# The third product ordered ahead of a chunk's sums, and a new order for a layer's first step, in a three-layer WKV kernel with a graph convolution

## The chip, the cores and the metric

The kernel runs on one core of one Trainium2 chip. The metric is the time of one execution on the device, in microseconds. Five engines work beside each other, each through its own queue of instructions in order: TensorE (PE in the profile) multiplies matrices, VectorE (DVE) and GpSimd (POOL) work elementwise, ScalarE (ACT) evaluates functions, SyncE (SP) issues the transfers. An engine waits on semaphores where it needs another's result.

## The reference, cut to what matters

The input x has 16 images of 192 channels and 56 x 56 positions, in 32-bit floats. Three layers of the first kind follow each other, then one convolution layer. All four add their result to x, and all start with a group norm (32 groups of 6 channels).

```python
# one layer of the first kind; xs is the normed x as tokens (T = 3136) by channels
k = xs @ Wk.T; v = xs @ Wv.T; r = xs @ Wr.T
x_fwd = wkv_scan(-exp(w_decay), u, k, v)            # over the tokens, forwards
x_bwd = flip(wkv_scan(-exp(w_decay), u, flip(k), flip(v)))   # and backwards
h = sigmoid(r) * 0.5 * (x_fwd + x_bwd)
h = (h - mean(h)) * rsqrt(var(h) + 1e-5) * ln_g + ln_b       # over the channels
x = x + h @ Wo.T

# wkv_scan, in the form without the running maximum:
#   q_t = d * q_{t-1} + e^{k_t};  p_t = d * p_{t-1} + e^{k_t} v_t    (d = e^w)
#   y_t = (p_t + c e^{k_t} v_t) / (q_t + c e^{k_t})

# the last layer
m = max(x[2 up] - x, x[2 down] - x, x[2 left] - x, x[2 right] - x, 0)
x = x + gelu(batch_norm(conv_w @ concat(x, m) + conv_b))
```

## The kernel before, in words

**Tiling.** Two images make a pair: 2 x 192 channels are three blocks of 128 rows (the middle one holds the remaining 64 channels of both images). The tokens are cut into seven chunks of 448. So a tile of a chunk is 128 x 3 x 448. The tiles live in 33 slots that are handed out and given back in program order. Matrix results live in seven PSUM banks, which are handed out in the same way. A product of a 384-channel chunk with a weight matrix (`project`, L597 to L607) takes three banks.

**Two passes.** A layer goes over its pair twice. The pass forwards (unit "A") does, for a chunk: k (`a_keys`), e^k (`a_exp`), v (`a_values`), e^k v (`a_ekv`), the scans of q and p (`a_q`, `a_p`, L875), the bonuses, which add c e^k and c e^k v (`a_den`, `a_num`, L890), the inverse of the denominator as ln and exp(-.) on ScalarE (`invert`, L975 and L978), and y on POOL (`a_y`, L982). The pass backwards (unit "B") takes the chunks from the last to the first: scans (`b_q`, `b_p`), bonuses (`b_den`, `b_num`, L890), inverse, and on POOL the mix (`b_mix`, L1031 to L1033, nine multiplies and adds, three for each block), which joins both directions and multiplies by sigmoid(r). For the sigmoid, r is a product (`b_gate`), then e^-r on ScalarE (`b_exp`, L996), then ln and exp (`b_sigmoid`, L1003 and L978).

**The layer norm behind the mix**, for a chunk: squares on ScalarE (`b_squares`, L1040); sums over the channels as matmuls into one bank (`b_sums`, L1047 for the outer blocks, L1049 for the middle one); the squared mean on ScalarE (`b_rs1`, L1055); its subtraction as a matmul (`b_rs2`, L1059); ln and exp on ScalarE (`b_rs3`, L1063 and L1065); the spreading of the result over the rows by matmul (`b_spread`, L1071); the scaling on VectorE (`b_scale`, L1076); the product with Wo (`b_out`, "ops"); its addition to x (`b_x`, L1089) and a store; and the statistics for the next layer's norm on ScalarE (`b_stats`, L734 and L735).

**Order of the work.** The order of each engine's queue is that of the program: the whole is under a manual schedule. Two streams of pairs are interlaced, so that in most steps the backward chunk of one pair and the forward chunk of the other are worked on together. A list of 249 steps is made, and each calls one function:

- `both_a`, here called a joint step, 85 times: a backward chunk b and a forward chunk a. A chunk's layer norm is spread over two steps: squares, sums and L1055 at the end of a joint step, L1059 on in the next one.
- `both_a_first`, the opening step, 17 times: the first such step after the turn between two layers. It finishes the layer norm of the last chunk before it in full, and begins that of its own.
- `forward_a` and `backward_alone`, at the turn between layers. In `backward_alone` stands `gap(G)`, which takes the next part of the following layer's group norm from a list: here `norm_fold`, four small operations on POOL, and the folding of the norm into the weights of k and v on ScalarE (L770).
- `both_c` (42) and `forward_c`: the same with the convolution, in 7 groups of six `both_c` each.

One opening step and the five joint steps after it are called a group here. There are 17. In nine of them the steps also carry the count of statistics of the input of later pairs (`count`: one or two blocks per step, two passes of ScalarE with an accumulation each, L734 and L735): these are called counting groups, the other eight quiet groups.

**Where r stands.** A step gets the next step's backward chunk as `nback` and calls `b_gate(nback)` and then `b_exp(nback)`; in `both_a` these are the first two calls. So TensorE's queue in a joint step is: r, L1059, v, L1071, ops, k, sums. ScalarE's queue, from the sums on, is: L1055, ln and exp of q (`invert(den())`), then the next step's e^-r, counting, the saving of a column (`b_q`, L884), L1063, L1065, sigmoid, the inverse of b's denominator, statistics, squares and e^k.

Of the kernel before, what the change touches and what calls it, by code (L numbers as in the profile page):

```python
# [55 lines left out]
NL = T // L  # L56
# [417 lines left out]
def fast_path(ctx: ExitStack, tc: tile.TileContext, flag, x, wproj, wfold, wcfold, wconst, wgroup, sums, picks, vecs, out):  # L474
# [374 lines left out]
    def product(run, what, w, xs, first):  # L849

        ps = run.ps[what] = banks(what)
        n = L + 1 if first else L
        project(ps, w, lambda rows, j: xs.full[rows, j, 0:n], n)
# [81 lines left out]
    def a_ekv(run, c):  # L935
        if c == 0:
            take_bias(run, "v", V)
        e, ps, b = slot_of(run.ekv, c, "ekv"), run.ps["v"], run.bias["v"]
        for j in ORDER:
            V.scalar_tensor_tensor(e.t[:, j, :], ps[j][:, 0:L], b[:, j, :], run.ek[c].t[:, j, :], ALU.add, ALU.mult)  # L940
            release(ps[j])

    def a_q(run, c):
        if once(run, "q", c):
            run.den[c] = scan(run, "q", run.ek[c], AHEAD, c == 0)
# [38 lines left out]


    def b_gate(run, c):
        product(run, "r", run.w[2], run.xb[c], c == NL - 1)

    def b_exp(run, c):
        if c == NL - 1:  # L990
# [21 lines left out]
    def b_den(run, c):  # L1012
        q = run.q.pop(c)
        bonus(run, run.ek[c], run.ek[c], q)
        q.give(V)

    def b_p(run, c):
        if c not in run.p:
            run.p[c] = scan(run, "p", run.ekv[c], BACK, c == NL - 1)
            if c > 0:  # L1020
                save(run.p[c], BACK, run.ekv[c - 1])
# [15 lines left out]
    def b_squares(run, c, js=ORDER):  # L1037
        h, sq = run.h[c].t, run.ek[c].t
        for j in js:
            S.activation(sq[:, j, :], h[:, j, :], AF.Square)  # L1040

    def b_sums(run, c):
        h, sq = run.h[c].t, run.ek.pop(c)
        st = run.ps["st"] = bank("st")
        parts = ((h, 0), (h, 1), (sq.t, 0), (sq.t, 1))
        for n, (t, i) in enumerate(parts):
            PE.matmul(st[32 * n : 32 * n + 32, :L], ones[:, 0, :], t[:, 2 * i, :], start=True, stop=False)  # L1047
        for n, (t, i) in enumerate(parts):
            PE.matmul(st[32 * n : 32 * n + 32, :L], ones[:, 1 + i, :], t[:, 1, :], start=False, stop=n < 2)  # L1049
        sq.give(PE)  # L1050

    def b_rs1(run, c):
        rs, st = row.tile([P, L], F32, tag="rs", name=name("rs")), run.ps["st"]
        run.rs[c] = rs
        S.activation(rs[LO, :], st[LO, :L], AF.Square)  # L1055

    def b_rs2(run, c):

        PE.matmul(run.ps["st"][HI, :L], pick[LO, 0, 0:64], run.rs[c][LO, :], start=False, stop=True)  # L1059
# [260 lines left out]
        for _ in range(min(most, len(z))):  # L1320
            z_stats(*z.pop(0))

    def both_a(b, a, nback, nfront, z, loads):

        den = lambda: a[0].den[a[1]]
        l = of_stage(0.5)
        load_ahead(nback)
        store()
        if nback is not None:
            b_gate(*nback[1:])  # L1330
            b_exp(*nback[1:])
        count(z)
        b_q(*b)
        if l:
            b_rs2(*l)
            b_rs3(*l)
        b_sigmoid(*b)
        a_values(*a)
        if l:
            b_spread(*l)  # L1340
        b_p(*b)
        b_den(*b)
        for js in (AC, slice(1, 2)):
            ln(b[0].ek[b[1]], js)
            exp_minus(b[0].ek[b[1]], js)
        b_num(*b)
        b_mix(*b)
        for u in loads:
            load_ahead(u)
        if l:  # L1350
            b_scale(*l)
            b_out(*l)
            late[l] = 2
        a_ekv(*a)
        sum_up()
        keys(nfront)
        a_q(*a)
        if l:
            add(l)
        b_squares(*b, (0,))  # L1360
        a_save(*a)
        count(z)
        exp_keys(nfront, (0, 2))
        b_squares(*b, (2,))
        exp_keys(nfront, (1,))
        b_squares(*b, (1,))
        b_sums(*b)
        a_p(*a)
        gap()
        a_den(*a)  # L1370
        b_rs1(*b)
        late[b] = 0.5
        invert(den())
        gap()
        a_num(*a)
        a_y(*a)
        gap()

    def both_a_first(b, a, nback, nfront, loads):

        den = lambda: a[0].den[a[1]]
        l = of_stage(0)
        load_ahead(nback)
        store()
        a_values(*a)
        b_squares(*l, (0, 2))
        b_q(*b)
        b_sigmoid(*b)
        b_p(*b)
        b_den(*b)  # L1390
        invert(b[0].ek[b[1]])
        b_num(*b)
        b_mix(*b)
        for u in loads:
            load_ahead(u)
        a_ekv(*a)
        b_squares(*l, (1,))
        if nback is not None:
            b_gate(*nback[1:])
        b_sums(*l)  # L1400
        b_rs1(*l)
        if nback is not None:
            b_exp(*nback[1:])
        a_q(*a)
        b_rs2(*l)
        b_rs3(*l)
        keys(nfront)
        a_p(*a)
        spread_and_scale(l)
        b_squares(*b, (0,))  # L1410
        a_save(*a)
        exp_keys(nfront)
        b_squares(*b, (2, 1))
        b_sums(*b)
        a_den(*a)
        b_rs1(*b)
        late[b] = 0.5
        invert(den())
        a_num(*a)
        add(l)  # L1420
        a_y(*a)
# [245 lines left out]
    def backward_alone(b, nback, nfront):  # L1667
        load_ahead(nback)
        load_ahead(nfront)
        store()  # L1670
        sum_up()
        b_q(*b)
        gap()
        b_den(*b)
        gap()
        invert(b[0].ek[b[1]])
        b_sigmoid(*b)
        b_p(*b)
        gap(G)
        b_num(*b)  # L1680
        b_mix(*b)
        for u in list(late):
            finish(u)
        if nback is not None:
            b_gate(*nback[1:])
            b_exp(*nback[1:])
        keys(nfront)
        exp_keys(nfront)
        late[b] = 0
# [13 lines left out]
    with tc.manual_schedule(engines={PE.engine, V.engine, S.engine, G.engine, nc.sync.engine}):  # L1703
        S.preload_act_table_set(TABLES)
        first = chains[0][0]
        for c in range(NL):
            load_ahead(("Z", first, c))
        for c in range(NL):
            count([(first, c, j) for j in ORDER], 3)
        for i, (b, f, z) in enumerate(steps):  # L1710
            nback, nfront, _ = steps[i + 1] if i + 1 < len(steps) else (None, None, None)
            for run in starts.get(i, ()):
                begin_later(run)
            if i == 0:
                keys(f)
                exp_keys(f)
            ahead = [("Z", run, c) for run, c, _ in (z if not b else [])]
            ahead += [nfront] if b and f else []
            ahead += [("Z", run, c) for run, c, _ in (steps[i + 1][2] if i + 1 < len(steps) else [])]
            ahead += [steps[i + 2][0]] if i + 2 < len(steps) else []  # L1720

            nkeys = nfront if nfront is not None and nfront[0] == "A" else None
            if f and not b and nkeys is None and nfront is not None and i + 2 < len(steps):
                far = steps[i + 2]
                if far[0] is None and far[1] is not None and far[1][0] == "A" and far[1][1] is f[1]:
                    nkeys = far[1]
            if f and nback is None and nfront is not None:
                near = [u for _, u, _ in steps[i + 1 : i + 4] if u is not None and u[0] == "A"]
                if len(near) > 1 and near[1][1] is near[0][1]:
                    ahead.append(near[1])  # L1730
            if not (b and f):
                for u in ahead:
                    load_ahead(u)
            if b and f and f[0] == "A":
                if of_stage(0) is None:
                    both_a(b[1:], f[1:], nback, nfront, z, ahead)
                else:
                    both_a_first(b[1:], f[1:], nback, nfront, ahead)
            elif b and f:
                both_c(b[1:], f[1:], nback, nfront, ahead)  # L1740
            elif f and f[0] == "A":
                forward_a(f[1:], nback, nfront, nkeys, z)
            elif f:
                forward_c(f[1:], nback, nfront)
            elif b:
                backward_alone(b[1:], nback, nfront)
            else:
                neither(nback, nfront)
            assert not z
        store()  # L1750
        assert not late and not unsummed and not convs and not half
# [100 lines left out]
```

## Time and profile before

| | us |
|---|---|
| median of 3 runs | 5206.31 |
| lowest and highest | 5205.58, 5208.39 |
| the profiled execution | 5220.16 |
| its span, first to last instruction | 5218.2 |

| steps of one group, from the start of the backward scan of q on VectorE | quiet group, us | counting group, us |
|---|---|---|
| opening step | 30.5 | 30.5 |
| first joint step | 25.7 | 27.0 |
| second, third, fourth | 23.6, 23.6, 23.6 | 26.6, 27.2, 27.2 |
| fifth | 24.3 | 24.2 |

The mean granted TensorE clock is 0.935 of full speed. A line of the timeline has the start in us, the duration in us from the first to the last of the instructions merged in it, the engine, the line of the program, the operation, out<-in, the sizes, and in brackets the idle time of the engine before it and what ended that. A line of the windows view has a stretch of the span, its length, the busy time of each engine with the number of its instructions, the granted share of TensorE's clock (PEclk), and the share of the DMA engines. An engine that is never idle in a step sets the step's length; where none is, the step is set by a loop through several engines.

### The profile page before, as it was taken

How to read it: one execution, taken by the hardware profiler on the slowest of the kernel's cores; microseconds unless marked ns; L12 is line 12 of the kernel's file. 1: busy time of each engine (PE TensorE's matmuls, PEld its weight loads, DVE VectorE, ACT ScalarE, POOL GpSimd, SP SyncE). 2: the span in 40 equal slices, each digit the busy share in tenths (PEclk: the TensorE clock that was granted, in tenths of full speed). 3: DMA queues.
4: the chain of work that ended last, by engine and by line, in shares of the span. 5: the costliest groups of instructions: out<-in, count | busy, mean ns of one | idle time of the engine just before them, and what ended most of it. 6: DMA issues, size and time to landing. Idle time of an engine off the chain costs nothing. (4 is left out here: it accounts for less than half of the span.)

```text
span 5218.2 us, 51856 instructions
## 1 busy us (share of the span) xinstructions
PE 4733.3 (91%) x15542; PEld 1498.8 (29%) x15542; DVE 4750.5 (91%) x6271; ACT 3684.6 (71%) x7163; POOL 2889.2 (55%) x2251
## 2 busy tenths in 40 slices
PE   7899998989899999998989999999898999999897
PEld 3222222223232222222323222222232322222222
DVE  6999999998989999999898999999889899999995
ACT  6777787776566777787656678777756667777772
POOL 1665665554545656565454556556545455666562
PEclk8999999999899999999989999999998999999998
DMA  5222222233232222223233223222333322222233
GB/s 154 69 82 87 90 86 89 85 110 97 90 116 72 87 90 93 82 90 122 93 93 101 84 75 100 88 85 87 128 93 101 93 74 77 72 84 77 80 104 120
DMA packets 314274, 482.47 MB, mean 92 GB/s; under 512 B 66432, under 2 KB 306688, under 8 KB 313984
## 3 DMA queue, kind: packets, MB, share of 16 engines
q1 hardware_dynamic: 312832, 477.59, 28.5%
q8 instruction: 126, 2.06, 0.2%
q10 hardware_dynamic: 1152, 1.48, 0.1%
q14 instruction: 164, 1.34, 0.1%
HBM read 324.83 MB, written 154.14 MB: 92 GB/s over the span
## 5 line engine op out<-in xcount | busy, mean ns | idle before, releaser
L875 DVE TENSOR_TENSOR_SCAN q<-fdecays,ek 128x449 f32<-128x449 f32 (+1 forms) x1008 | 1023.4, 1068 | 28.0 <-ACT ek L920 25.4
L875 DVE TENSOR_TENSOR_SCAN p<-fdecays,ekv 128x449 f32<-128x449 f32 (+1 forms) x1008 | 1020.3, 1065 | 0.6
L982 POOL TENSOR_TENSOR p<-p,q 128x1344 f32<-128x1344 f32 x168 | 512.0, 3047 | 830.3 <-ACT q L978 546.9
L1031 POOL TENSOR_TENSOR ekv<-ekv,ek 128x448 f32<-128x448 f32 x504 | 602.7, 1196 | 456.1 <-ACT ek L978 385.3
L1033 POOL TENSOR_TENSOR p<-p,sg 128x448 f32<-128x448 f32 x504 | 638.0, 1266 | 57.2 <-ACT ek L884 12.7
L1032 POOL TENSOR_TENSOR p<-p,ekv 128x448 f32<-128x448 f32 x504 | 606.1, 1203 | 39.5
L1040 ACT ACTIVATE ek<-p 128x448 f32<-128x448 f32 x504 | 286.4, 572 | 309.4 <-POOL p L1033 308.9
L886 POOL COPY ekv<-p 128x3 f32<-128x3 f32 x282 | 233.1, 827 | 488.0 <-DVE p L875 457.2
L1076 DVE TENSOR_TENSOR p<-p,rsb 128x448 f32<-128x448 f32 x504 | 282.4, 613 | 194.5 <-PE rsb L1071 194.4
L920 ACT ACTIVATE ek<-k,k 128x448 f32<-128x448 f32 x504 | 297.2, 632 | 225.3 <-PE k L601 179.2
L735 ACT ACTIVATE fjunk<-x 128x448 f32<-128x448 f32 x672 | 387.7, 577 | 40.1 <-DVE x L1089 13.4
L1071 PE MATMUL rsb<-rs,fpicks 32*128 32x448 f32 (+1 forms) x1008 | 359.2, 629 | 42.4 <-ACT rs L1065 42.4
L1159 POOL TENSOR_TENSOR ml<-ml,x 128x1344 f32<-128x1344 f32 x56 | 178.9, 3194 | 391.8 <-ACT ml L1150 391.8
L890 DVE SCALAR_TENSOR_TENSOR ek<-ek,fcc,q 128x896 f32<-128x896 f32 x336 | 379.1, 1167 | 0.0
L890 DVE SCALAR_TENSOR_TENSOR q<-ek,fcc,q 128x896 f32<-128x896 f32 x336 | 359.2, 1109 | 6.3 <-ACT cvb L954 4.6
L1089 DVE SCALAR_TENSOR_TENSOR x<-ops,fwob,x 128x448 f32<-128x448 f32 x504 | 314.2, 670 | 46.7 <-PE ops L601 26.6
L734 ACT ACTIVATE fjunk<-x 128x448 f32<-128x448 f32 x600 | 342.5, 571 | 11.4
L996 ACT ACTIVATE sg<-r,r 128x448 f32<-128x448 f32 x504 | 313.0, 627 | 33.5 <-PE r L607 20.7
L890 DVE SCALAR_TENSOR_TENSOR ekv<-ekv,fcc,p 128x896 f32<-128x896 f32 x336 | 330.1, 1022 | 0.0
L940 DVE SCALAR_TENSOR_TENSOR ekv<-v,v,ek 128x448 f32<-128x448 f32 x504 | 312.5, 672 | 16.6 <-PE v L601 8.0
L975 ACT ACTIVATE q<-q 128x1344 f32<-128x1344 f32 x168 | 221.5, 1318 | 125.5 <-DVE q L890 101.3
L890 DVE SCALAR_TENSOR_TENSOR p<-ekv,fcc,p 128x896 f32<-128x896 f32 x336 | 295.3, 919 | 6.5 <-POOL ekv L886 1.7
(235 smaller groups left out, 11546.4 us busy)
## 6 DMA issues: line engine op xcount, KB each, us to landing
x<-xd SPq DMA_DIRECT2D x240, 672.0 KB, 5.3
xd<-x SPq DMA_DIRECT2D x168, 672.0 KB, 3.9
x<-in_x_dram SPq DMA_DIRECT2D x320, 224.0 KB, 4.3
x<-in_x_dram SPq DMA_DIRECT2D x320, 112.0 KB, 4.2
out_dram<-ml SPq DMA_DIRECT2D x112, 224.0 KB, 2.3
m<-xd SPq DMA_DIRECT2D x112, 168.0 KB, 5.1
wkv<-in_wfold_dram SPq DMA_DIRECT2D x24, 640.0 KB, 5.6
out_dram<-ml SPq DMA_DIRECT2D x112, 112.0 KB, 2.3
```

Source lines behind the costliest of these rows:

```text
L734: S.activation(junk, xt[:, j, :], AF.Identity, accum_out=stats[:, 0, j, c : c + 1])
L735: S.activation(junk, xt[:, j, :], AF.Square, accum_out=stats[:, 1, j, c : c + 1])
L875: V.tensor_tensor_scan(out, dec[:, column(j)].to_broadcast([P, L if first else L + 1]), e, 0.0, ALU.mult, ALU.add)
L890: by_channel(lambda js, i: V.scalar_tensor_tensor(dst.t[:, js, :], e.t[:, js, :], cc[:, i : i + 1], state.t[:, js, :], ALU.mult, ALU.add))
L940: V.scalar_tensor_tensor(e.t[:, j, :], ps[j][:, 0:L], b[:, j, :], run.ek[c].t[:, j, :], ALU.add, ALU.mult)
L982: G.tensor_mul(run.h[c].t, run.h[c].t, den.t)
L996: S.activation(sg.t[:, j, :], ps[j][:, 0:L], AF.Exp, bias=b[:, j, :], scale=-1.0, accum_out=run.chk[:, at : at + 1])
L1031: G.tensor_mul(y.t[:, j, :], y.t[:, j, :], den.t[:, j, :])
L1032: G.tensor_add(h.t[:, j, :], h.t[:, j, :], y.t[:, j, :])
L1033: G.tensor_mul(h.t[:, j, :], h.t[:, j, :], sg.t[:, j, :])
L1071: PE.matmul(ps[j][:, :L], pick[rows, j, :], rs[rows, :], start=True, stop=True)
L1089: V.scalar_tensor_tensor(xj, ps[j][:, 0:L], wob[:, column(j)], xj, ALU.add, ALU.add, accum_out=run.new[:, 0, j, c : c + 1] if c == 0 else ...
```

## The change

No operation is added or taken away. Four things change places.

1. In `both_a` and `both_a_first`, the product r of the backward chunk two steps on (`far`, if it is of the same layer and pair) is put just ahead of the step's own sums. The next step's call of `b_gate` then does nothing for it, since `once` remembers it. Each group's r of four chunks is concerned; the r that the opening step makes for its own `nback` stays where it was.
2. In the opening step, `a_q` and `a_ekv` (with the squares of the middle block after them) go ahead of the bonuses of the backward chunk.
3. Also there, L1059 to L1065 (`b_rs2`, `b_rs3`) go ahead of e^-r, the saving of q's column ahead of `a_p`, and spreading, scaling and ops (`spread_and_scale`) ahead of k (`keys`).
4. In `backward_alone`, `gap(G)` goes from behind sigmoid and the scan of p to ahead of both.

In the main loop a name is changed (`then`) and `far` is worked out. All lines from L988 on move down by one, those after the opening step by more.

```diff
     def b_gate(run, c):
-        product(run, "r", run.w[2], run.xb[c], c == NL - 1)
+        if once(run, "r", c):
+            product(run, "r", run.w[2], run.xb[c], c == NL - 1)
...
-    def both_a(b, a, nback, nfront, z, loads):
+    def both_a(b, a, nback, nfront, z, loads, far):
...
         exp_keys(nfront, (1,))
         b_squares(*b, (1,))
+        if far:
+            b_gate(*far[1:])
         b_sums(*b)
         a_p(*a)
...
-    def both_a_first(b, a, nback, nfront, loads):
+    def both_a_first(b, a, nback, nfront, loads, far):
...
         b_q(*b)
         b_sigmoid(*b)
         b_p(*b)
+        a_q(*a)
+        a_ekv(*a)
+        b_squares(*l, (1,))
         b_den(*b)
         invert(b[0].ek[b[1]])
         b_num(*b)
         b_mix(*b)
         for u in loads:
             load_ahead(u)
-        a_ekv(*a)
-        b_squares(*l, (1,))
         if nback is not None:
             b_gate(*nback[1:])
         b_sums(*l)
         b_rs1(*l)
+        b_rs2(*l)
+        b_rs3(*l)
         if nback is not None:
             b_exp(*nback[1:])
-        a_q(*a)
-        b_rs2(*l)
-        b_rs3(*l)
-        keys(nfront)
+        a_save(*a)
         a_p(*a)
         spread_and_scale(l)
+        keys(nfront)
         b_squares(*b, (0,))
-        a_save(*a)
         exp_keys(nfront)
         b_squares(*b, (2, 1))
+        if far:
+            b_gate(*far[1:])
         b_sums(*b)
         a_den(*a)
         b_rs1(*b)
...
         invert(b[0].ek[b[1]])
+        gap(G)
         b_sigmoid(*b)
         b_p(*b)
-        gap(G)
         b_num(*b)
         b_mix(*b)
...
+            far = steps[i + 2][0] if nback is not None and i + 2 < len(steps) else None
+            if far is not None and far[1] is not nback[1]:
+                far = None
             if b and f and f[0] == "A":
                 if of_stage(0) is None:
-                    both_a(b[1:], f[1:], nback, nfront, z, ahead)
+                    both_a(b[1:], f[1:], nback, nfront, z, ahead, far)
                 else:
-                    both_a_first(b[1:], f[1:], nback, nfront, ahead)
+                    both_a_first(b[1:], f[1:], nback, nfront, ahead, far)
```

More of the change, by code (lines that the diff above doesn't have):

```diff
@@ L1723, in fast_path @@
             if f and not b and nkeys is None and nfront is not None and i + 2 < len(steps):
-                far = steps[i + 2]
-                if far[0] is None and far[1] is not None and far[1][0] == "A" and far[1][1] is f[1]:
-                    nkeys = far[1]
+                then = steps[i + 2]
+                if then[0] is None and then[1] is not None and then[1][0] == "A" and then[1][1] is f[1]:
+                    nkeys = then[1]
             if f and nback is None and nfront is not None:
```

## The prediction

> **What bounds the kernel now.** I read the page's busy times first, then busy time step by step, then the timelines of one quiet step, one counting step and one opening step. The page:
>
> ```profile
> PE 4733.3 (91%) x15542; PEld 1498.8 (29%) x15542; DVE 4750.5 (91%) x6271; ACT 3684.6 (71%) x7163; POOL 2889.2 (55%) x2251
> ```
>
> Two engines at 91% can't say which one sets a step. The windows view, cut where VectorE starts its first backward scan of a step, does: a quiet joint step, the opening step, and the first and third joint step of a counting group.
>
> ```profile
> core 0: us, PE busy (x) PEld busy (x) DVE busy (x) ACT busy (x) POOL busy (x), PEclk, DMA share, GB/s
> 412.50:436.10 23.60, 23.29 (x82) 7.15 (x84) 23.60 (x31) 19.25 (x38) 15.32 (x12) 1.00 0.27 89
> ...
> 512.80:543.30 30.50, 28.37 (x110) 8.97 (x110) 27.14 (x32) 19.86 (x40) 23.39 (x24) 1.00 0.02 7
> 543.30:570.30 27.00, 24.91 (x88) 7.57 (x82) 25.65 (x30) 21.59 (x46) 17.67 (x15) 0.95 0.38 128
> ...
> 596.90:624.10 27.20, 25.11 (x82) 7.64 (x80) 25.09 (x31) 21.59 (x45) 15.67 (x12) 0.94 0.22 77
> ```
>
> A quiet joint step is full on VectorE (23.60 of 23.60) and all but full on TensorE: nothing can be won there, only lost. A counting step has 2.1 us free on both: a loop through several engines sets it. The loop, in the quiet step's timeline:
>
> ```profile
> 409.15 0.94 PE L1049 MATMUL st<-p,fsums 128*32 128x448 f32 x4 [0.30 <-POOL p L1033]
> ...
> 410.63 1.02 PE L598 MATMUL r<-x,wr 128*128 128x448 f32 x2
> 410.75 0.54 ACT L1055 ACTIVATE rs<-st 64x448 f32<-64x448 f32 x1 [1.05 <-PE st L1049]
> ...
> 413.77 0.62 ACT L996 ACTIVATE sg<-r,r 128x448 f32<-128x448 f32 x1
> ...
> 415.14 0.96 PE L1059 MATMUL st<-rs,fpicks 64*64 64x448 f32 x2
> ...
> 416.80 0.57 ACT L1065 ACTIVATE rs<-rs 64x448 f32<-64x448 f32 x1
> ...
> 420.54 1.97 PE L1071 MATMUL rsb<-rs,fpicks 32*128 32x448 f32 x6
> ...
> 421.99 1.14 POOL L1031 TENSOR_TENSOR ekv<-ekv,ek 128x448 f32<-128x448 f32 x1 [2.42 <-ACT ek L978]
> ...
> 422.43 1.02 PE L598 MATMUL ops<-p,fwo 128*128 128x448 f32 x2
> ```
>
> Sums, then r (4.51 us, 410.63 to 415.14), then L1059. While r runs, ScalarE does L1055, ln and exp of q, and e^-r, all ahead of L1063 and L1065. So r hides that chain from TensorE. The mix of POOL then runs 421.99 to 432.7 and ends as VectorE starts its bonuses. In a counting step 1.4 us of counting stands on ScalarE in this loop, and the mix comes later:
>
> ```profile
> 565.65 2.59 DVE L890 SCALAR_TENSOR_TENSOR q<-ek,fcc,q 128x896 f32<-128x896 f32 x2
> 565.73 2.04 POOL L1033 TENSOR_TENSOR p<-p,sg 128x448 f32<-128x448 f32 x1
> ...
> 567.82 0.96 PE L1049 MATMUL st<-p,fsums 128*32 128x448 f32 x2 [2.09 <-POOL p L1033]
> ```
>
> The bonus takes 2.59 where it took 1.72 in the quiet step (409.18), the POOL multiply 2.04 where it took 1.15. TensorE waits 2.09, and then runs at half clock:
>
> ```profile
> 567.70:571.10 3.40, 3.28 (x10) 1.00 (x11) 3.32 (x4) 1.50 (x3) 3.40 (x5) 0.50 0.01 2
> ```
>
> Last, the opening step:
>
> ```profile
> 518.72 3.15 DVE L890 SCALAR_TENSOR_TENSOR ek<-ek,fcc,q 128x896 f32<-128x896 f32 x2
> ...
> 536.63 1.68 DVE L1076 TENSOR_TENSOR p<-p,rsb 128x448 f32<-128x448 f32 x3 [3.36 <-PE rsb L1071]
> ```
>
> Bonuses doubled by the mix beside them, then 3.36 us of waiting for the spreading, which stands behind k (4.5 us) on TensorE.
>
> [...]
>
> **The change part by part.** No instruction is added or removed; only order changes. Times inside a joint step are counted from the start of ops.
>
> *r ahead of the sums, joint steps.* TensorE's order becomes rs2, v, spreading, ops, k, r, sums. ops, k and r are 13.53; the sums unbroken take 1.78 to L1055 (527.81 to 529.59 in the opening step): L1055 at 15.31. From there ScalarE needs 3.02 to e^-r (410.75 to 413.77), 1.85 for that, 1.48 for saving and L1063/L1065: 6.35, now with only rs2 and v (5.5) to cover it. Then 1.11 to the scaling (spreading to first scaling 1.05) and 0.73 to ops: 23.50 a step, beside VectorE's 23.58. But the mix starts 4.62 after L1065 (393.81 to 398.43), which is 2.8 after ops where it was 0.4 before ops, and takes 10.66: it ends at 13.4, and the bonuses start at 10.31 (scaling 398.12 to bonus 409.18, less 0.73). So 3.1 us of mix lies on them. From the counting step, 1.15 of POOL work beside a bonus costs VectorE 0.87 and POOL 0.89, so I take 0.75 per us on VectorE and, with 0.5 in the opening step (1.87, 1.52, 1.88 and 1.41 for four times 1.14), 0.65 on POOL. Settling the period against this overlap: 25.8, 25.5, 25.2 in the second to fourth step, for 23.58: over the group +1.9, +1.6, +1.2. Lower bound: no collision, 23.58. Counting steps: 1.41 more in the chain, collision full, the mix ends at 15.4, L1055 at 17.1, period 17.1+6.35+1.41+1.84 = 26.7 for 26.6, 27.2, 27.2: -1.1 over three steps; without collision 24.9. The waits left (0.7, 1.7, 1.0) are shorter than 2.09, so I give the clock back. The fourth step has no r left; its mix sets it still. Fifth: 0 quiet, +1.7 counting (mix now on the bonuses).
>
> *Banks and loads.* The moved r takes banks freed by b_x and by e^k, both done before k ends; its x is loaded some 15 us ahead. Nothing, either way at most 0.5.
>
> *Folding ahead of p.* k starts 2.75 after r because the fold (1.73) stands behind two sigmoid passes (2.67). Now k starts at 511.5, not 514.3; sigmoid is 1.7 later, POOL needs it at 515.2 as it comes.
>
> *Opening step.* v ends at 521.0; r, sums to 527.2. The scan of q and e^k v now stand ahead of the bonuses on VectorE, which are then free of the mix (-3.2) but end b_den at 525.6 for 521.9. Its ln/exp on ScalarE ends 528.3, and L1055 stands behind it: rs2 528.8, L1065 531.05, scaling 532.2 for 536.6, ops 532.9 for 537.5. Then k, and r of two chunks on: 546.5, sums, L1055 548.3 (before 543.8, with that r after it). L1065 of the next step: 554.65, scaling 555.8 (counting 557.2) for 554.6. With the mix then on its bonuses (+2.2) the first joint step ends 572.5 for 569.0: +3.5 quiet, 573.9 for 570.3: +3.6 counting. VectorE's own gain of 2.4 in the opening step is spent in waiting there.
>
> *Convolution groups.* The same fold move lets mix and sums come about 1.4 earlier in the first step of 7 groups: -10.
>
> *Sum.* 8 quiet groups: 3.5+1.9+1.6+1.2 = 8.2, 66. 9 counting groups: 3.6-1.1+1.7 = 4.2, 38. Less 10: +94 on the profiled 5220.2 (span 5218.2), thus 5314 there. The median is 5206.3, 0.27% lower: 5300.
>
> **Rivals.** (a) The collision doesn't come, because VectorE's pace lets the mix slip ahead again. For it: before, the mix ended just where the bonuses began. Against: the mix hangs on L1065, as the scaling does, so it can't gain on ops. Then quiet groups lose 1.3 (10), counting ones gain 5.5 (50), folding 10: 5156. It decides from an overlap below some 1 us a step. (b) TensorE's new waits in counting groups pull the clock to half in four steps each: 4x9x1.7 = 61 more, 5360. Against: each is shorter than 2.09. (c) Gain and loss meet, overlap about half of mine: 5206 within 0.2%, for which 10 us is what a measurement of this kernel can tell.
>
> **How the numbers follow.** Forecast 0.62, (a) 0.20, (b) 0.10, (c) 0.08. Slower 0.72, same 0.08, faster 0.20. The likeliest one's own range is 5240 to 5340; with (b), (c) and part of (a) 5170 to 5360.
>
> **What would show it.** Right: quiet joint steps of about 25 us with bonuses (L890) of 2.3 to 2.9 beside L1034, the new name of L1033; gaps on TensorE before rs2 (0.7) and before the spreading; first joint steps with several us of VectorE idle ahead of the scaling; PEclk at 1.00 in counting steps. Wrong: quiet steps still at 23.6, or counting ones below 25.5.

## The result, and the profile after

| | us |
|---|---|
| before, median | 5205.94 (5199.82 to 5208.39) |
| after, median of 4 runs | 5411.84 (5405.23 to 5422.42) |
| ratio, with its 95% interval | 1.0399 (1.0380 to 1.0418) |
| span of the profiled execution, before and after | 5218.2, 5409.3 |

The change makes the kernel 206 us slower. The forecast was 94 us slower, and 5411.84 lies outside its range of 5170 to 5360. The busy line of the page after:

```profile
PE 4794.1 (89%) x15542; PEld 1516.8 (28%) x15542; DVE 4828.1 (89%) x6271; ACT 3671.6 (68%) x7163; POOL 2840.4 (53%) x2251
```

Same instructions, but VectorE is busy 78 us longer (4750.5 before) and TensorE 61 us (4733.3 before): part of the loss is work that runs slower, the rest is waiting. POOL is busy for less time (2889.2 before).

The profiled execution of the kernel before was 14 us longer than its median, which is why the spans differ by 191 us and the medians by 206. Cutting both traces at the start of the backward scan of q, step by step, shows where the 191 us are. The table gives after minus before for one group, as a mean over the 8 quiet and the 9 counting groups, beside the prediction's own terms.

| step | quiet, measured | quiet, predicted | counting, measured | counting, predicted |
|---|---|---|---|---|
| opening and first joint step | +0.9 and +7.9 | +3.5 | +1.0 and +8.7 | +3.6 |
| second, third and fourth | +0.7, +3.8, +3.1 | +1.9, +1.6, +1.2 | -0.6, -0.1, +0.5 | -1.1 together |
| fifth | -0.4 | 0 | +0.4 | +1.7 |

The groups make +218 (8 x 16.0 and 9 x 9.9); the convolution steps give back 11.6, the forward steps at the turns 15.4. So the first joint steps alone hold 63.5 + 78.5 = 142, more than the whole forecast.

The windows view of after, from the start of one step to that of the next: the third and fourth quiet step; an opening step, and the stretch in the middle of it; the first joint step behind it; then the second to fifth joint step of that counting group together.

```profile
435.60:462.90 27.30, 24.59 (x83) 7.61 (x84) 27.30 (x30) 19.03 (x37) 15.18 (x12) 0.94 0.23 76
462.90:489.90 27.00, 22.08 (x88) 6.25 (x84) 27.00 (x30) 20.44 (x39) 15.22 (x12) 1.00 0.21 71
...
541.60:572.50 30.90, 27.72 (x84) 8.77 (x84) 24.83 (x33) 17.06 (x33) 21.72 (x21) 0.83 0.13 45
...
558.60:568.80 10.20, 9.14 (x15) 3.16 (x16) 4.15 (x6) 3.61 (x10) 9.74 (x10) 0.50 0.00 0
...
572.50:607.30 34.80, 31.96 (x120) 9.49 (x116) 25.41 (x31) 24.61 (x52) 16.52 (x15) 1.00 0.30 100
...
607.30:712.20 104.90, 94.03 (x300) 29.16 (x300) 101.54 (x118) 85.55 (x176) 61.77 (x48) 0.90 0.28 92
```

The quiet steps are again full on VectorE, 27.00 of 27.00, with the same operations that took 23.60 before: its operations have become slower. The opening step has a stretch of 10.2 us in which TensorE is granted half its clock (0.83 over the step, 1.00 before), and VectorE is busy only 24.83 of 30.90. In the first joint step VectorE is idle for 9.4 us.

The timeline of the fourth quiet step, with the lines of VectorE's slow operations and of what set their neighbours:

```profile
458.75 2.61 DVE L890 SCALAR_TENSOR_TENSOR q<-ek,fcc,q 128x896 f32<-128x896 f32 x2
...
465.25 0.54 ACT L1056 ACTIVATE rs<-st 64x448 f32<-64x448 f32 x1 [4.83 <-PE st L1050]
465.69 1.31 ACT L975 ACTIVATE q<-q 128x1344 f32<-128x1344 f32 x1
...
467.04 1.33 ACT L978 ACTIVATE q<-q 128x1344 f32<-128x1344 f32 x1
...
468.50 3.05 POOL L982 TENSOR_TENSOR p<-p,q 128x1344 f32<-128x1344 f32 x1 [7.69 <-ACT q L978]
...
468.85 4.24 DVE L890 SCALAR_TENSOR_TENSOR ek<-ek,fcc,q 128x896 f32<-128x896 f32 x2
...
476.18 1.14 POOL L1032 TENSOR_TENSOR ekv<-ekv,ek 128x448 f32<-128x448 f32 x1 [3.64 <-ACT ek L978]
...
485.72 2.65 DVE L890 SCALAR_TENSOR_TENSOR q<-ek,fcc,q 128x896 f32<-128x896 f32 x2
```

The denominator of q was ready at 461.36 (458.75 + 2.61), yet its inverse (L975, L978) starts at 465.69: it stands behind L1056, which waits 4.83 for the sums, because r now runs ahead of them. The inverse sets POOL's y (L982), which at 468.50 falls on the backward bonuses. They take 4.24 where they took 1.71 before. The mix (L1032) comes late as well, behind sigmoid and the inverse in ScalarE's queue, and makes the forward bonuses 2.65 long. In the kernel before, in the same step (it begins at 436.06), y ran beside the two scans and was over before the bonuses began:

```profile
437.56 3.05 POOL L982 TENSOR_TENSOR p<-p,q 128x1344 f32<-128x1344 f32 x1 [3.64 <-ACT q L978]
439.02 3.02 DVE L875 TENSOR_TENSOR_SCAN p<-fdecays,ekv 128x449 f32<-128x449 f32 x3
441.98 1.71 DVE L890 SCALAR_TENSOR_TENSOR ek<-ek,fcc,q 128x896 f32<-128x896 f32 x2
```

The opening step of a counting group and the start of the next, in the timeline:

```profile
555.57 1.33 ACT L978 ACTIVATE ek<-ek 128x1344 f32<-128x1344 f32 x1
556.80 0.52 ACT L1056 ACTIVATE rs<-st 64x448 f32<-64x448 f32 x1
...
557.38 0.96 PE L1060 MATMUL st<-rs,fpicks 64*64 64x448 f32 x2 [1.86 <-ACT rs L1056]
...
559.66 3.72 PE L1072 MATMUL rsb<-rs,fpicks 32*128 32x448 f32 x6 [1.32 <-ACT rs L1066]
...
563.32 1.86 PE L598 MATMUL ops<-p,fwo 128*128 128x448 f32 x2
...
566.38 0.21 ACT L884 ACTIVATE ek<-q 128x3 f32<-128x3 f32 x1 [4.79 <-POOL p L1033]
...
589.97 1.69 DVE L1077 TENSOR_TENSOR p<-p,rsb 128x448 f32<-128x448 f32 x3 [8.22 <-PE rsb L1072]
```

L1056 starts as the inverse ahead of it ends, 1.3 after the sums. TensorE waits 1.86 for it, does L1060, and waits again, 1.32, since k no longer stands between L1060 and the spreading. From there it runs at half clock: the spreading takes 3.72 instead of 1.97, ops 7.2 (563.32 to 570.52) instead of 4.58, some 4.3 us lost. Then come k, r and the sums, so in the next step VectorE waits 8.22 for its scaling.

### The profile page after: what moved, and what is told of

The parts are those of the page before. It is cut to its first block, busy times and chain, and to the rows that moved or that the text cites. A ratio compares the mean times of both kernels' runs of the same rounds, so it can differ in the third digit from the quotient of the medians.

```text
span 5409.3 us, 51930 instructions
## 1 busy us (share of the span) xinstructions
PE 4794.1 (89%) x15542; PEld 1516.8 (28%) x15542; DVE 4828.1 (89%) x6271; ACT 3671.6 (68%) x7163; POOL 2840.4 (53%) x2251
## 5 line engine op out<-in xcount | busy, mean ns | idle before, releaser
L982 POOL TENSOR_TENSOR p<-p,q 128x1344 f32<-128x1344 f32 x168 | 519.4, 3091 | 1082.0 <-ACT q L978 776.6
L875 DVE TENSOR_TENSOR_SCAN p<-fdecays,ekv 128x449 f32<-128x449 f32 (+1 forms) x1008 | 1022.3, 1070 | 43.2 <-PE st L1050 42.6
L875 DVE TENSOR_TENSOR_SCAN q<-fdecays,ek 128x449 f32<-128x449 f32 (+1 forms) x1008 | 1024.7, 1072 | 23.5 <-ACT ek L920 20.9
L1032 POOL TENSOR_TENSOR ekv<-ekv,ek 128x448 f32<-128x448 f32 x504 | 598.6, 1188 | 512.3 <-ACT ek L978 428.0
L1034 POOL TENSOR_TENSOR p<-p,sg 128x448 f32<-128x448 f32 x504 | 614.2, 1219 | 59.0 <-ACT sg L978 13.9
L1033 POOL TENSOR_TENSOR p<-p,ekv 128x448 f32<-128x448 f32 x504 | 618.1, 1226 | 39.5
L1072 PE MATMUL rsb<-rs,fpicks 32*128 32x448 f32 (+1 forms) x1008 | 391.5, 673 | 131.8 <-ACT rs L1066 131.8
L890 DVE SCALAR_TENSOR_TENSOR q<-ek,fcc,q 128x896 f32<-128x896 f32 x336 | 411.9, 1267 | 39.0 <-ACT ek L884 34.4
L890 DVE SCALAR_TENSOR_TENSOR ek<-ek,fcc,q 128x896 f32<-128x896 f32 x336 | 430.6, 1322 | 0.0
L886 POOL COPY ekv<-p 128x3 f32<-128x3 f32 x282 | 202.4, 718 | 317.7 <-DVE p L875 300.5
L890 DVE SCALAR_TENSOR_TENSOR p<-ekv,fcc,p 128x896 f32<-128x896 f32 x336 | 297.4, 927 | 44.5 <-POOL ekv L886 41.3
L598 PE MATMUL ops<-p,fwo 128*128 128x448 f32 x336 | 233.3, 785 | 113.1 <-DVE p L1077 112.6
L940 DVE SCALAR_TENSOR_TENSOR ekv<-v,v,ek 128x448 f32<-128x448 f32 x504 | 312.8, 675 | 11.6 <-PE v L601 8.0
L1060 PE MATMUL st<-rs,fpicks 64*64 64x448 f32 x336 | 174.4, 601 | 151.5 <-ACT rs L1056 142.6
```

The source lines that it names most:

```text
L875: V.tensor_tensor_scan(out, dec[:, column(j)].to_broadcast([P, L if first else L + 1]), e, 0.0, ALU.mult, ALU.add)
L890: by_channel(lambda js, i: V.scalar_tensor_tensor(dst.t[:, js, :], e.t[:, js, :], cc[:, i : i + 1], state.t[:, js, :], ALU.mult, ALU.add))
L982: G.tensor_mul(run.h[c].t, run.h[c].t, den.t)
L1032: G.tensor_mul(y.t[:, j, :], y.t[:, j, :], den.t[:, j, :])
L1033: G.tensor_add(h.t[:, j, :], h.t[:, j, :], y.t[:, j, :])
L1034: G.tensor_mul(h.t[:, j, :], h.t[:, j, :], sg.t[:, j, :])
```

## The experiments

Each was compared with the kernel before on the same chip, and the ratio to that is given with its 95% interval. Differences by step are taken from the profiled spans.

### The parts by themselves

The changed kernel without part 1 (r where it was):

```diff
-        if far:
-            b_gate(*far[1:])
         b_sums(*b)
```

> The changed kernel with r where it was before (parts 2, 3 and 4 alone). Theory A: the opening step's new order makes TensorE wait twice (1.86 and 1.32 us) and so run spreading and ops at half clock, whatever r does; the first joint step then comes some 4.3 us late in each of 17 groups (73 us) less some 10 us for the fold: about 5270 us, with spreading near 3.7 us and ops near 7.2 us in the opening step. Theory B: r ahead of the sums is the whole cost: 5190 us or less, with spreading near 2.0 and ops near 4.6 us.

Measured: 5290.97, 1.0142 (1.0118 to 1.0167). Its windows: a quiet joint step, an opening step, and 10.2 us in the middle of that.

```profile
423.90:447.40 23.50, 23.21 (x82) 7.07 (x82) 23.50 (x30) 19.24 (x37) 15.29 (x12) 1.00 0.27 87
523.00:553.90 30.90, 27.70 (x84) 8.69 (x84) 24.81 (x33) 17.10 (x33) 21.75 (x21) 0.83 0.14 45
...
539.90:550.10 10.20, 9.00 (x15) 3.02 (x16) 4.15 (x6) 3.75 (x10) 9.74 (x10) 0.50 0.00 0
```

Without the moved r, quiet joint steps are back at 23.6, but the half clock in the opening step is there as in the changed kernel. So the half clock comes from the opening step's new order, the long quiet steps from r. First joint steps are still 5.0 (quiet) and 5.9 (counting) longer than before. Theory B falls.

Part 1 alone, on the kernel before (the `far` lines of both step functions and of the main loop, `once` in `b_gate`, nothing else):

> The kernel before with r of two chunks on ahead of the sums alone (part 1). Theory A: r costs 3.5 us in the first joint step (no half clock, as the old opening step has no two waits) and what the later joint steps of the changed kernel show (7.6 us in quiet groups, about 0 in counting ones): 8 x 11 + 9 x 3.5, about 5320 us. Theory B, r is the whole cost: 5410 us.

Measured: 5312.75, 1.0186 (1.0161 to 1.0210). The window of a fourth quiet step of it:

```profile
454.90:481.90 27.00, 23.65 (x88) 6.75 (x84) 27.00 (x30) 20.47 (x39) 15.23 (x12) 0.94 0.22 70
```

It has the 27.0 of the changed kernel, and its opening step keeps most of its clock (0.95 over the step). Its first joint steps are 4 longer. So r costs by itself some 2%, and theory B falls here too.

Part 4 alone (the fold of the norm ahead of sigmoid and p):

```diff
+        gap(G)
         b_sigmoid(*b)
         b_p(*b)
-        gap(G)
```

> The kernel before with the folding ahead of sigmoid and p alone (part 4). The steps of the convolution and the forward steps behind them lose 27 us in the changed kernel; if the fold does this, about 5180 to 5190 us. If the fold only moves k ahead of work that sets the pace anyway: 5206 us.

Measured: 5165.48, 0.9897 (0.9870 to 0.9924). This part is a gain of 54.5 on the spans, more than either expectation: 20.4 in the opening steps, of which many are 29.5 long instead of 30.5, some 10 in the joint steps, 12.4 in the convolution groups and 14.2 in the forward steps at the turns. The last two aren't shown to be the fold's: in the run of part 1 alone, which has no fold, the convolution groups are 6.3 and the forward steps 17.3 shorter than in the same trace of the kernel before.

On the spans, the fold is worth -54.5, r by itself +87.8 (5306.0), parts 2 and 3 +127.3 (5291.0 against 5163.7). That is +160.6, and 30.5 less than the change. They aren't a cost of the parts' meeting each other: within the groups the fold is worth -30.6, r +113.7, parts 2 and 3 +134.7, together 217.8, and the changed kernel has 217.6. The 30.5 lie outside the groups, in convolution steps and turns, where the trace of the kernel before is longer than those of all the other runs, so that much the same 25 us are counted as a gain of the fold and again as a gain of r.

### What costs in the opening step

The changed kernel, with r moved in joint steps only:

```diff
         b_squares(*b, (2, 1))
-        if far:
-            b_gate(*far[1:])
         b_sums(*b)
```

> The changed kernel with r moved in the joint steps alone, not in the opening step. Theory A: the half clock in the opening step costs its 4.3 us a group, the later joint steps of quiet groups 7.6 us a group: 5206 + 73 + 61 - 10, about 5330 us. Theory B, the r in the opening step is what delays the first joint step: 5206 + 61 - 10, about 5257 us.

Measured: 5359.42, 1.0277 (1.0252 to 1.0303), 58 less than the changed kernel on the spans. First joint steps become 2.8 shorter per group: r ahead of the opening step's sums delays L1056, L1060 and the spreading. Quiet third and fourth steps stay at 25.3 to 27.1, and second ones become longer (26.4 for 24.3). Theory B falls: the r of joint steps costs without that of the opening step.

The changed kernel, with k ahead of the spreading as it was before:

```diff
-        spread_and_scale(l)
         keys(nfront)
+        spread_and_scale(l)
```

> The changed kernel with k put back ahead of the spreading in the opening step, so that TensorE has 4.5 us of work while L1056 to L1066 run on the other engines. Theory A, half clock from two waits: spreading 2.0 and ops 4.6 us again, the sums of the opening step 5.6 us earlier, 17 x 5.4 = 92 us: about 5320 us. Theory B, the r ahead of the sums makes the first joint step late by itself: 5400 us.

Measured: 5356.70, 1.0309 (1.0292 to 1.0326), between the two. The waits of TensorE in the opening step's timeline, L1060 and the spreading:

```profile
550.94 0.96 PE L1060 MATMUL st<-rs,fpicks 64*64 64x448 f32 x2 [1.86 <-ACT rs L1056]
...
557.98 1.97 PE L1072 MATMUL rsb<-rs,fpicks 32*128 32x448 f32 x6
```

and the one stretch at half clock in this step, in the windows view:

```profile
552.60:556.00 3.40, 3.40 (x7) 0.84 (x5) 0.00 (x0) 2.53 (x7) 3.24 (x4) 0.50 0.00 0
```

The first wait is still 1.86, the second gone. A stretch of 3.40 at half clock is left, which falls on k; the spreading is back at 1.97, and PEclk of the step is 0.94 for 0.83. First joint steps are 4.4 shorter per group, 75 in all, but opening steps of six counting groups become 2.0 to 5.4 longer.

The same without r moved:

> The same k ahead of the spreading, with r where it was before. Theory A: no half clock is left and TensorE works without a long pause from v to the sums, 29.4 us from the start of the step as against 29.5 with the fold alone: 5165 us, give or take 15. Theory B, the scan and e^k v ahead of the bonuses cost by themselves, as L1056 stands behind a later inverse: 5220 us or more.

Measured: 5221.69, 1.0051 (1.0034 to 1.0068). So the swap of k and the spreading is worth 71.5 of the 127.3 (5291.0 to 5219.5). Quiet groups are now, in the mean, 0.6 us longer than in the kernel before, but in six of nine counting groups the opening step takes 36 to 38 us instead of 30 to 32. So the expected 5165 isn't reached, and theory B's number came: the scan ahead of the bonuses costs by itself. The next run isolates it, and shows that in those six steps the wait is another than B's.

Part 2 alone, on the fastest kernel of this study (`fold_count` below, span 5063.2):

```diff
         b_p(*b)
+        a_q(*a)
+        a_ekv(*a)
+        b_squares(*l, (1,))
         b_den(*b)
...
-        a_ekv(*a)
-        b_squares(*l, (1,))
...
-        a_q(*a)
```

> The fold and counting versions together (the fold ahead of sigmoid, counting behind the inverse; 5064.6), with part 2 of the change alone: in the opening step the scan of q and e^k v ahead of the bonuses. Theory A (the loss of the new opening step comes from part 3 alone, and part 2 frees the bonuses of the mix beside them): openings 0 to 2.4 shorter, 5025 to 5064. Theory B (part 2 itself costs: the bonuses end 3.7 later, the inverse of their denominator stands ahead of L1056 on ScalarE, L1060 comes late behind it and TensorE waits): openings 1 to 3 longer, 5080 to 5115.

Measured: 5149.84, 0.9892 (0.9875 to 0.9908), against 0.9742 (0.9726 to 0.9759) without it: 80 us on the spans from the scan's place alone. Theory A falls; the loss is more than B's range too. Opening steps of quiet groups lose 1.4 to 3.0, three of the counting ones 1.4 each, but the other six counting ones 9.8 each, 59 together. One of these in the timeline:

```profile
706.08 0.52 ACT L1055 ACTIVATE rs<-st 64x448 f32<-64x448 f32 x1
...
715.65 0.64 ACT L996 ACTIVATE sg<-r,r 128x448 f32<-128x448 f32 x1 [9.04 <-POOL p L1032]
...
718.91 3.65 PE L1071 MATMUL rsb<-rs,fpicks 32*128 32x448 f32 x6 [5.14 <-ACT rs L1065]
...
720.88 1.15 DVE L1076 TENSOR_TENSOR p<-p,rsb 128x448 f32<-128x448 f32 x2 [12.81 <-PE rsb L1071]
```

The same place in `fold_count`, where e^-r doesn't wait:

```profile
702.96 0.54 ACT L1055 ACTIVATE rs<-st 64x448 f32<-64x448 f32 x1 [1.04 <-PE st L1049]
703.40 0.62 ACT L996 ACTIVATE sg<-r,r 128x448 f32<-128x448 f32 x1
```

In `count_scan` ScalarE waits 9.04 with e^-r, and what releases it is POOL's last add of the mix (L1032, third block, 714.48 to 715.62), which neither reads r nor writes anything that e^-r needs as an input. It is the last to read e^k v of that chunk. What they share is a slot: slots are handed out in program order, and `a_q` and `a_ekv` have now been served first. Following the slots through the program shows it. In `count_scan` e^-r gets the slot of this mix's e^k v in exactly these six opening steps of the 17, the ones in which a third load takes a slot as well; in `fold_count` it gets another slot in all 17. L1063 and L1065 stand behind e^-r, the spreading behind them (it waits 5.14 and takes 3.65 for 1.97; the step's PEclk is 0.83, and 1.00 in `fold_count`), and VectorE waits 12.81. In the changed kernel, part 3 puts L1064 and L1066 ahead of e^-r; there the same wait (6.76 in the opening step from 739.3 on) holds up ops for 2.59 instead, and the slots are shared in the same six steps. The 1.4 us of the other opening steps fit theory B's later inverse, but no run isolates that.

The saving of a column had a wait of the same kind in the changed kernel (4.79 above, on the mix; its slot, too, is that of the mix's e^k v in this step):

```diff
-        a_save(*a)
         a_p(*a)
...
         b_squares(*b, (0,))
+        a_save(*a)
         exp_keys(nfront)
```

> The changed kernel, with the saving of q's column (L884) in the opening step back behind keys and the first squares, so that its slot is asked for later. Theory A (it gets the slot that the mix still reads, waits 4.88 us on ScalarE with e^k and squares behind it, and the bonuses of q wait 2.5 us for it): opening and first joint step together 1.5 to 2.5 us shorter in each of 17 groups, 5370 to 5385. Theory B (the wait is covered: with it gone the bonuses wait for something else as long, since TensorE at half clock sets the step): 5405 to 5415.

Measured: 5411.23, 1.0395 (1.0378 to 1.0412), no difference. This wait was covered: the opening step's length is set elsewhere, and a wait on the page was no loss.

### What costs in the joint steps

The changed kernel without the multiplication that makes y on POOL (L982), in joint steps only; its y is left as the numerator:

```diff
         a_num(*a)
-        a_y(*a)
+        a[0].den.pop(a[1]).give(G)
```

> The changed kernel without the multiplication of y (L982) in the joint steps: the numerator of the pass forwards stays undivided there, so the output is another one. Theory A, VectorE's bonus of 4.2 to 4.6 us in the third and fourth step of quiet groups is the collision with that multiplication: it falls to 1.7 us, the steps from 27.2 to some 24.5, 8 x 2 x 2.7: about 5365 us. Theory B, the chain through ScalarE sets these steps: they stay at 27 us, 5405 us.

Measured: 5375.39, 1.0336 (1.0319 to 1.0354). Windows of a third and a fourth quiet step:

```profile
431.21:458.25 27.04, 25.85 (x101) 7.68 (x100) 25.11 (x31) 19.21 (x38) 12.33 (x11) 1.00 0.24 77
458.25:482.80 24.55, 21.47 (x69) 6.30 (x69) 24.55 (x31) 20.35 (x39) 12.20 (x11) 0.93 0.24 79
```

The fourth step falls from 27.0 to 24.6, the third doesn't: there VectorE has 1.93 idle, and its forward bonuses still lie under a late mix (it runs to 456.41, and those of p wait 1.2 for POOL's copy behind it). So y on the bonuses is real, but it is one of two things; the late mix is the other.

Both could come from ScalarE's queue behind L1056. Two runs on that: first L1060, L1064 and L1066 ahead of the next step's e^-r:

```diff
+        if l:
+            b_rs2(*l)
+            b_rs3(*l)
         if nback is not None:
             b_gate(*nback[1:])
             b_exp(*nback[1:])
         count(z)
         b_q(*b)
-        if l:
-            b_rs2(*l)
-            b_rs3(*l)
```

> The changed kernel, with L1060, L1064 and L1066 ahead of the next step's e^-r in joint steps, so that ScalarE has 1.85 us less between the sums and L1066. Theory A (in joint steps the moved r takes away the cover of ScalarE's chain; L1066, the scaling and the mix that hangs on them come late by that chain): L1066 some 1.8 earlier, first joint steps 1.8 shorter, quiet third and fourth steps 25 to 25.5 for 27.3 and 27.0: 17x1.8 + 8x3.6 + some for counting groups, about 5330. Theory B (the order on TensorE alone decides, e^-r only moves its wait elsewhere): within 0.3% of the changed kernel, 5395 to 5425.

Measured: 5398.86, 1.0368 (1.0351 to 1.0385): 13 us lower in median, with intervals that overlap, and quiet steps still at 27.4 and 27.0. Theory A falls. Three lines of the fourth quiet step's timeline say why:

```profile
470.23 0.57 ACT L1066 ACTIVATE rs<-rs 64x448 f32<-64x448 f32 x1
470.83 0.64 ACT L997 ACTIVATE sg<-r,r 128x448 f32<-128x448 f32 x1
...
477.36 1.15 POOL L1032 TENSOR_TENSOR ekv<-ekv,ek 128x448 f32<-128x448 f32 x1 [3.63 <-ACT ek L978]
```

L1066 did come earlier, 6.0 after the step's start for 8.0. But the mix doesn't hang on it: it waits for the inverse of e^k, which stands behind sigmoid in ScalarE's queue, and e^-r, moved back, stands ahead of both. The mix starts 13.2 after the step's start, as in the changed kernel.

Then the changed kernel with the inverse of q ahead of L1056:

```diff
-        b_rs1(*b)
-        late[b] = 0.5
         invert(den())
+        b_rs1(*b)
+        late[b] = 0.5
```

> The changed kernel, with L1056 in joint steps behind ln and exp of q's denominator on ScalarE (2.6 us), which wait for the bonuses of q alone, not for the sums. Theory A (what r costs joint steps is ScalarE's queue behind L1056: the inverse of q comes late, so that POOL's y lies on the backward bonuses, and sigmoid and the inverse for the mix come late behind it): y then runs beside scans, the bonuses of e^k in quiet third and fourth steps fall from 4.2 to 4.6 to below 2, and these steps from 27.3 and 27.0 to 24.5 or less; 8x5 = 40 less in quiet groups and something in counting ones, 5340 to 5370. Theory B (TensorE's order sets these steps: sums behind r, then L1060 and the spreading): no change or, since L1056 can come later, slower: 5405 to 5440.

Measured: 5282.45, 1.0158 (1.0134 to 1.0182): 128 us less than the changed kernel on the spans (5281.2), of which 107 lie in the groups; far more than A's 40 to 70, and B falls. The timeline of a quiet step of it:

```profile
452.48 1.33 ACT L975 ACTIVATE q<-q 128x1344 f32<-128x1344 f32 x1 [1.02 <-DVE q L890]
...
455.08 0.52 ACT L1056 ACTIVATE rs<-st 64x448 f32<-64x448 f32 x1
...
455.31 3.04 POOL L982 TENSOR_TENSOR p<-p,q 128x1344 f32<-128x1344 f32 x1 [3.47 <-ACT q L978]
...
459.88 1.72 DVE L890 SCALAR_TENSOR_TENSOR ek<-ek,fcc,q 128x896 f32<-128x896 f32 x2
```

and the windows of that step, and of a fourth joint step of a counting group:

```profile
453.97:477.54 23.57, 19.88 (x78) 5.77 (x70) 23.57 (x31) 19.16 (x38) 15.28 (x12) 1.00 0.26 87
643.13:667.41 24.28, 19.58 (x74) 5.77 (x66) 24.28 (x30) 21.33 (x46) 15.25 (x12) 1.00 0.42 133
```

The inverse uses the time in which ScalarE waited for the sums; y is back beside scans, the backward bonuses at 1.72, the quiet second and fourth steps at 23.6 to 24.3 (four of the eight third ones still take 25.4). The second to fourth counting steps, 26.6 to 27.3 before the change, are now 24.3 to 25.2: r and that one swap together shorten the loop that set them. Whether the swap would do it without r wasn't run. What remains of the loss is in the opening and first joint steps, which didn't move.

### A version that beats both

The fold alone, with the first count of a joint step moved behind the inverse of the backward denominator, so that it no longer stands in the loop ahead of the mix:

```diff
-        count(z)
         b_q(*b)
...
         a_ekv(*a)
+        count(z)
         sum_up()
```

> The kernel before with the fold ahead of sigmoid and p, and the first counting of a joint step behind the inverse instead of ahead of the saving. If the loop over ScalarE and the mix sets the counting steps, 1.4 us of counting in it and the half clock behind it go, and they fall from 27 to some 24.5 us: 9 x 4 x 2.5 = 90 us, about 5075 us. If ScalarE's whole load sets them: 5165 us.

Measured: 5064.58, 0.9742 (0.9726 to 0.9759), the fastest kernel here. The third joint step of a counting group:

```profile
588.39:611.98 23.59, 23.59 (x82) 7.24 (x84) 23.59 (x31) 21.60 (x46) 15.33 (x12) 1.00 0.26 91
```

It took 27.2 before; it is now as full on VectorE and TensorE as a quiet one, and the clock is 1.00. The loop that r was meant to shorten could be shortened on ScalarE instead, without taking the cover from anything.

## Why the prediction was wrong

**The direction was right and so was the bound.** The reading that quiet steps had nothing to gain and that moving r would put POOL's work onto VectorE's bonuses holds: quiet third and fourth steps lie at 27 with VectorE full. Rival (a), that the collision doesn't come, and rival (c), that gain and loss meet, are out.

**The opening step failed, and most of the miss is there.** The step of the working was "rs2 528.8, L1065 531.05, scaling 532.2 for 536.6, ops 532.9 for 537.5", and 3.5 to 3.6 for it and the first joint step together. Measured are 8.8 and 9.7, and the difference over 17 groups is some 97 us, against 112 missing in the medians. On the scale of these figures (the step starts 28.8 us later in the new trace, which is taken off), the chain came as worked out up to L1066, which ends at 530.8. What failed is the term behind it, that spreading and ops run at their full pace: the spreading takes 3.72 for 1.97 and ops 7.2 for 4.58, so k begins at 541.6 where the sum has 537.4, and L1056 of the next chunk comes at 552.5 for 548.3. That is 4.2 us, or some 71 in 17 groups if each loses as much. Three things stand behind the miss:

- k, 4.5 us of work, was what TensorE did between L1060 and the spreading. The forecast took the earlier spreading as a gain and had no term for what TensorE does without k. It waits 1.86 and 1.32 and loses 4.3 to half clock. The runs with k put back are worth 72 and 55 us.
- Slots: "Banks and loads ... Nothing" looked at the moved r alone. Parts 2 and 3 also move who asks for a slot first. Part 2 alone costs 80 us in the run that isolates it, 59 of it in six steps with this wait. In the changed kernel the loss is smaller: the opening and first joint step together take 65.6 in three counting groups and 68.5 to 69.2 in the six.
- r ahead of the opening step's sums did have a term (L1055 at 548.3 for 543.8), and is a real delay: 2.8 per group in first joint steps.

**The collision had the right place, but half its sources.** The prediction laid the mix onto the forward bonuses (2.3 to 2.9 forecast, 2.61 and 2.65 measured). It missed y on the backward bonuses (4.2 to 4.6), because it followed the chain L1055 to L1065 and not the other work queued behind L1055: the inverse of q. So quiet second to fourth steps lost 7.6 and not 4.7, with a smaller loss in the second (0.7 for 1.9). The sum was also short by its own figures: 25.8, 25.5 and 25.2 against 23.58 are 2.2, 1.9 and 1.6, one us a group more, and three times 26.7 in counting groups is 0.9 less than before, not 1.1; some 10 us in all, a small part of the miss. The run with that inverse first takes back 128 us. It also shows the counting groups' gain, which the forecast put at 1.1 for three steps and which was 0.2: with that inverse out of the way it is 7.5 a group against the kernel before. That ScalarE takes its queue in order shows in L975 of the changed kernel: its input is ready at 461.36, and it starts at 465.69, behind L1056. This is the case that the forecast overlooked.

**"I give the clock back" was wrong.** The argument was that each wait is shorter than 2.09; it was the author's estimate, from the waits of 2.09 alone. The second to fifth joint steps of a counting group have a PEclk of 0.90, where 0.93 stood for the same steps before. In the third joint step the longest wait of TensorE ahead of the fall is 1.57 (the spreading, 641.50), and 3.40 us at a PEclk of 0.51 follow (643.90 to 647.30). In the opening step of the kernel before, TensorE waits 2.75 ahead of k (514.28), and has a PEclk of 1.00 from there to the step's end. Rival (b) named this, in the joint steps; the larger part came in the opening step, which it left out.

**The fold was too small.** It gains 20.4 in the opening steps by itself, for which the forecast had no term, and the changed kernel loses that again. That the convolution groups came close to "-10" (12.4 by itself, 11.6 in the changed kernel) is partly luck, since 6.3 come there without the fold.

**What it said would show it:** the gap ahead of L1060 (0.66 in the fourth quiet step), VectorE's idle time ahead of the scaling in the first joint step (8.22) and the longer L890 beside the mix came as forecast; quiet steps of about 25 us (24.3, 27.3 and 26.7 in the mean for the second to fourth) and a PEclk of 1.00 in counting steps didn't.

## What to carry to other kernels

Moving one product ahead on one queue can delay what stands behind its consumer on the next queue, not only the chain that one is looking at: list that queue to its end, here the inverse of q behind L1056 (4.33 us late, 461.36 to 465.69), and check whether something independent can pass the one that waits. Before taking a filler such as k from between two dependent matmuls, add the waits that are left (1.86 and 1.32 here) and price the clock (4.3), not only the wait. Where buffers are handed out in program order, moving one request changes the buffers of all requests after it, and a wait then shows up on an operation that has no data in common with its releaser.

## What the runs showed of the hardware

- TensorE's two waits of 1.86 and 1.32, with 0.96 of work between, go with 10.2 us at half clock (558.60 to 568.80), three times the 3.40 that follow a wait of 2.09 in the kernel before. With k behind the first wait, 3.40 us at half clock are left (552.60 to 556.00), and the spreading has its full pace, 1.97.
- VectorE's bonuses of e^k take 4.24 beside one POOL multiply of 128 x 1344, and 1.71 without. The two share 2.70 us (468.85 to 471.55), and VectorE loses 2.53; this POOL multiply isn't slowed (3.05, as in the quiet step before). VectorE's scans aren't slowed either: the 2016 scans (L875) of the kernel before take 1.05 to 1.09 us each, those beside POOL among them, and the same number in the changed kernel 1.06 to 1.11.
